# Two layers of a vision network on one core: attention sums two steps per instruction, normalized x kept in DRAM, weight loads regrouped over two queues

## The chip, the core and the metric

The kernel runs on one core of a Trainium2 chip. A core has five engines that run their own instruction streams: TensorE (PE in the profile; PEld is its weight load), VectorE (DVE), ScalarE (ACT), GpSimd (POOL) and SyncE (SP). SyncE, and also ScalarE, start transfers on DMA queues. Each queue's issuing engine works in order: an issue that waits for a semaphore holds back what stands behind it on that engine. SBUF is the on-chip memory, PSUM is where TensorE writes. The metric is the device time of one execution in microseconds; lower is better.

## The reference, cut to what matters

The input x is 2 images of 96 channels and 96 x 96 pixels, float32. Layer 0 is a selective scan (a state-space block) and a small feed-forward net, layer 1 is an attention and a feed-forward net. The change touches layer 0 only in how its weights are loaded. In layer 1 the attention counts:

```python
# layer 1, per image
xn = _ln_c(x)                       # normalized over the 96 channels
kv = einsum('oc,bchw->bohw', kv_w, xn)      # keys and values of all 9216 pixels
x_samp = mean of xn over 2 x 2 pixels       # 48 x 48 = 2304 cells
q_samp = einsum('oc,bchw->bohw', q_w, x_samp)
attn = softmax(k^T q * scale, over the 9216 pixels)   # 3 heads of 32
distribution = v attn                        # 96 x 48 x 48
lepe = depthwise 5 x 5 convolution of v + lepe_b
dmat = softmax(x_unfold . samp_unfold * dist_scale)   # each pixel, 3 x 3 cells
feature = dmat . unfold3(distribution)
x = x + proj_w (feature + lepe) + proj_b
x = x + ffn(layernorm(x))                    # quantized weights, relu
```

Of layer 0's weights, three matter here: dt_projs_bias (4 directions x 192 channels), A_logs (4 x 192 channels x 16 states) and dt_projs_weight.

## The kernel before, in words

**Order of work.** `_layer0` runs the whole first layer for both images and writes its result to the DRAM tile `x2d`. `_layer1` then takes one image after the other through three stages: `_l1_before` (norm, keys, queries, values), `_l1_attention` (which runs `_l1_packed`, or an arm that shifts the scores where a bound on them is large, which is not taken here), and `_l1_rows` (local 5 x 5 convolution, the 3 x 3 cells, projection, feed-forward net), eight times 12 rows. Pools are opened at the start of a stage and closed at its end; a pool that is opened later may lie on the memory of a closed one and then waits for its last readers.

**The planner.** Layer 0, the norm stage and the rows stage are written as operations with a cost, tiles read and written and a due time, and `_Plan` sorts them by list scheduling; `_in_order` then pins the issue order on every engine, SyncE included. DMA issues are operations of engine "sp" there. The attention is written out by hand, and only TensorE's order is pinned.

**The weights (`_l0_weights`).** SyncE issues every load in the order of the text: in_proj, off1, out_proj, norm weights, x_proj; then, for each of the four directions, two loads of dt_w (lines 323 and 324) and six of `dt_b`, 32 values each, straight into their interleaved places (lines 330 and 333); then 16 copies of A_logs into the DRAM tile `ad` (L381), one for each state, four reads of `ad` into `at0`, and Ds. VectorE reorders the reads of `ad` into `at` and TensorE transposes it (`pa`). VectorE also builds `selb`, `w_bc` and others from the identity and x_proj. Then `_layer0` opens its pools in the order front, hand, rep, back and the first load of x (`xt`, L464) is issued; the front's first matmul is `axc` (L475).

**The norm stage (`_l1_before`).** For each of 16 stripes of six rows SyncE loads x2d into `xt` (three buffers), TensorE, ScalarE and VectorE normalize it (`nxc`, `nva`, `rs`), and VectorE writes the result into its place in `xn`, an SBUF tile of the whole image (96 x 9216) that lives until the rows stage ends. Keys (`pk`), values (`pv`), queries (`pq`) and the 2 x 2 means (`xs`, GpSimd) are computed from it.

**Attention (`_l1_packed`).** The 48 x 48 cells go in five chunks: four of ten rows (480 cells), one of eight (384). The 72 blocks of 128 keys are spread over four strips of 32 partitions: strips 0 to 2 take the three heads' blocks 18 to 71 (54 steps), strip 3 takes the first 18 blocks of head 0, then of head 1, then of head 2 (18 steps each, index p). So a step has four score matmuls (L1382) into two PSUM tiles `sc`, two exponentials on ScalarE (L1386) into the SBUF tile `pr` of 4 x 480, four value matmuls (L1443) that add up in `av`, and on VectorE one addition of `pr` to `sums` (L1456). The order on TensorE is: scores of step j + 1, then values of step j. The first step of a chunk is a copy instead (L1451); the first step of p = 1 and p = 2 adds three strips and copies the fourth; the last step of each p adds strip 3's sums to those of head p. The closing of a chunk (`close`, a generator) is threaded into the next chunk's steps:

```python
            if rest and j in (2, 6):
                next(rest)
```

Ahead of step 0 ScalarE copies `av` to `avs`; at step 2 three matmuls with ones add the sums over the 128 partitions and VectorE takes the reciprocal; at step 6 five matmuls join strip 3's values to the heads and VectorE multiplies into `dist`.

**The rows stage (`_l1_rows`).** For 12 rows, `q` from 0 to 7: values again from `xn` (`pv2`, rows two above to two below), the score of each pixel with its cells (`st`, from `xs` and `xn`, L1574 to 1578), the exponentials multiplied by a mask on GpSimd, 20 taps of the 5 x 5 convolution on VectorE (`acc`, L1615) and five on TensorE, projection and feed-forward net, and on SyncE the loads of `xr` and the stores of `out`.

## Time and profile before

| What | us |
|---|---|
| three runs: median (lowest to highest) | 8884.31 (8876.86 to 8887.73) |
| the profiled execution | 8876.68 |
| its span, first to last instruction | 8874.9 |
| layer 0 with its weights | 0 to 6786 |
| image 0: norm stage, attention, rows stage | 6786 to 6862, to 7488, to 7830 |
| image 1: norm stage, attention, rows stage | 7830 to 7908, to 8535, to 8875 |
| busy over the span: TensorE, VectorE, ScalarE, GpSimd | 7426.3, 8093.4, 6381.7, 6189.7 |
| GpSimd and VectorE in layer 0, largest groups: h (L1050), h (L1045), bp (L1030) | 4120.9, 3998.7, 2173.8 |

The mean granted TensorE clock is 0.893 of full speed. The profile also gives: the span in 40 slices with the busy share of each engine, the chain of waits that ended last, groups of instructions by line (count, busy time, mean time of one, idle time ahead of them and who ended it), the same by stretch of time, and timelines. In a group "out<-in" are the program's tile names; "<-ACT pr L1386 3.3" says that 3.3 us of the idle time ahead of the group were ended by ScalarE's instruction on line 1386. In a table by stretch each engine has its busy time and its number of instructions.

### The profile page before, as it was taken

How to read it: one execution, taken by the hardware profiler on the slowest of the kernel's cores; microseconds unless marked ns; L12 is line 12 of the kernel's file. 1: busy time of each engine (PE TensorE's matmuls, PEld its weight loads, DVE VectorE, ACT ScalarE, POOL GpSimd, SP SyncE). 2: the span in 40 equal slices, each digit the busy share in tenths (PEclk: the TensorE clock that was granted, in tenths of full speed). 3: DMA queues.
4: the chain of work that ended last, by engine and by line, in shares of the span. 5: the costliest groups of instructions: out<-in, count | busy, mean ns of one | idle time of the engine just before them, and what ended most of it. 6: DMA issues, size and time to landing. Idle time of an engine off the chain costs nothing. (4 is left out here: it accounts for less than half of the span.)

```text
span 8874.9 us, 120352 instructions
## 1 busy us (share of the span) xinstructions
PE 7426.3 (84%) x43537; PEld 3500.8 (39%) x43537; DVE 8093.4 (91%) x5663; ACT 6381.7 (72%) x10720; POOL 6189.7 (70%) x3931
## 2 busy tenths in 40 slices
PE   6788888888788888888888888888856999989998
PEld 3333334444343344434444433443423333543345
DVE  2999999999999999999999999999996998969988
ACT  4677777777777777777777777777754876677766
POOL 3999999988999889899898889898974001310022
PEclk9899889999988888889898988888956999999999
DMA  2444444444444444444444444444441000010000
GB/s 77 140 143 145 148 142 143 145 142 140 144 142 141 147 142 144 142 146 143 143 142 144 144 139 143 144 140 144 144 131 55 2 2 5 24 28 3 2 10 24
DMA packets 335667, 969.48 MB, mean 109 GB/s; under 512 B 50424, under 2 KB 52144, under 8 KB 334768
## 3 DMA queue, kind: packets, MB, share of 16 engines
q1 hardware_dynamic: 335056, 961.64, 34.2%
q8 instruction: 346, 5.67, 0.3%
q14 instruction: 265, 2.17, 0.1%
HBM read 788.04 MB, written 132.17 MB: 104 GB/s over the span
## 5 line engine op out<-in xcount | busy, mean ns | idle before, releaser
L1050 POOL TENSOR_TENSOR h<-h,cre 128x864 f32<-128x864 f32 x2048 | 4120.9, 2021 | 684.6 <-DVE h L1045 488.5
L1045 DVE TENSOR_TENSOR_SCAN h<-dA,bp 128x864 f32<-128x864 f32 x2048 | 3998.7, 1953 | 83.5 <-PE y L1062 5.4
L1010 ACT ACTIVATE dA<-dlr,A 128x576 f32<-128x576 f32 x3072 | 2156.5, 765 | 1102.2 <-DVE h L1045 1015.6
L1030 DVE TENSOR_TENSOR bp<-dur,B 128x864 f32<-128x864 f32 x2048 | 2173.8, 1061 | 282.2 <-DMA dur<-du_d 42.3
L1062 PE MATMUL y<-h,fold 128*32 128x288 f32 (+2 forms) x18432 | 1870.3, 452 | 167.5 <-POOL h L1050 158.1
L1025 PE MATMUL B<-bt,selb 128*128 128x288 bf16 x2048 | 642.4, 315 | 957.6 <-DVE bp L1030 945.7
L536 PE MATMUL pc<-xin,off 96*96 96x288 f32 x4608 | 1331.0, 416 | 1.0 <-ACT xin L501 0.9
L1062 PEld LDWEIGHTS y<-h,fold 128*32 128x32 f32 x18432 | 762.2, 119 | 1140.4 <-issue 549.6
L1386 ACT ACTIVATE pr<-sc 128x960 f32<-128x960 f32 (+1 forms) x1080 | 955.1, 936 | 255.6 <-DVE sums L1456 144.5
L1456 DVE TENSOR_TENSOR sums<-sums,pr 128x1920 f32<-128x1920 f32 (+1 forms) x510 | 1059.2, 2077 | 58.2 <-ACT pr L1386 7.1
L1537 POOL MEMSET vch<- 96x32 f32 x16 | 2.0, 124 | 1313.8 <-DVE dist L1415 1265.8
L536 PEld LDWEIGHTS pc<-xin,off 96*96 96x96 f32 x4608 | 714.1, 166 | 506.3 <-issue 260.7
L1025 PEld LDWEIGHTS <-selb 128*128 128x128 bf16 x2048 | 200.6, 99 | 1312.3 <-DVE bp L1030 805.8
L1382 PE MATMUL sc<-qH,kH 32*128 32x480 f32 (+1 forms) x3240 | 708.3, 602 | 8.9 <-DMA q<-qH 8.9
L1382 PE MATMUL sc<-q,kH 32*128 32x480 f32 (+1 forms) x1080 | 564.5, 602 | 0.0
L1443 PE MATMUL av<-pr,vT 128*32 128x480 f32 (+1 forms) x4320 | 533.3, 564 | 3.8 <-ACT av L1460 3.5
L1615 DVE SCALAR_TENSOR_TENSOR acc<-vch,lepe_w,acc 96x1152 f32<-96x1152 f32 x304 | 485.7, 1598 | 7.6
L1382 PEld LDWEIGHTS sc<-qH,kH 32*128 32x128 f32 x3240 | 284.5, 184 | 437.5 <-issue 303.0
L709 PE MATMUL pt<-xd,w_dt 96*128 96x288 f32 x768 | 317.7, 507 | 22.9 <-ACT zs L519 10.6
L728 POOL TENSOR_TENSOR e<-e,du 128x576 f32<-128x576 f32 x192 | 271.1, 1412 | 26.6 <-ACT du L724 26.5
L1580 POOL TENSOR_TENSOR e<-e,mask 100x384 f32<-100x384 f32 x96 | 169.0, 1781 | 172.4 <-ACT e L1578 172.1
L730 POOL TENSOR_TENSOR dl<-dl,r 128x576 f32<-128x576 f32 x192 | 270.6, 1410 | 6.2
(260 smaller groups left out, 10113.7 us busy)
## 6 DMA issues: line engine op xcount, KB each, us to landing
cre<-c_d SPq DMA_DIRECT2D x1024, 288.0 KB
dur<-du_d SPq DMA_DIRECT2D x256, 864.0 KB
dlr<-dl_d SPq DMA_DIRECT2D x256, 864.0 KB
x<-xs SPq DMA_DIRECT2D x512, 72.0 KB
du_d<-du SPq DMA_DIRECT2D x128, 288.0 KB
dl_d<-dl SPq DMA_DIRECT2D x128, 288.0 KB
du_d<-du SPq DMA_DIRECT2D x128, 144.0 KB
dl_d<-dl SPq DMA_DIRECT2D x128, 144.0 KB
```

What stands on the lines that cost most here:

```text
L536: pe(H2, lambda: nc.tensor.matmul(pc.ap[:C, :H2], k.w_c1[:, ih, tap, oh * C : (oh + 1) * C], xin.ap[:, ih, 3 * c + dy : 3 * c + dy + 3, dx ...
L1010: nc.scalar.activation(dA.ap[:, :, blk, :], dlr.ap[:, blk, :].rearrange("p (c n) -> p c n", c=2), AF.Exp, scale=k.A[:, i, kg, h, blk : blk ...
L1025: nc.tensor.matmul(pB.ap[:, :H2], k.selb[:, kk, i, :], f.bc[o].ap[:, toks], start=True, stop=True)
L1030: nc.vector.tensor_tensor(bp.ap[:, : NBL * H2].rearrange("p (b n) -> p b n", b=NBL), dur.ap[:, :, toks], pB.ap[:, :H2].unsqueeze(1).to_bro ...
L1045: nc.vector.tensor_tensor_scan(hv, dv, bv, 0.0, ALU.mult, ALU.add)
L1050: nc.gpsimd.tensor_tensor(ht.ap, ht.ap, cre.ap[:, toks].unsqueeze(1).to_broadcast([128, NBL, H2]), ALU.mult)
L1062: nc.tensor.matmul(dst, k.fold, v, start=False, stop=stop)
L1382: nc.tensor.matmul(two[s // 2][:, s % 2, :n], kH[rows, k0 : k0 + 128], q, start=True, stop=True)
L1386: nc.scalar.activation(pr[:, 2 * i : 2 * i + 2, :n], two[i][:, :, :n], AF.Exp, scale=HD**-0.5)
L1443: nc.tensor.matmul((main if s < HEADS else other)[s * HD : (s + 1) * HD, :n], vT[:, blk, hd, :], pr[:, s, :n], start=at == 0, stop=at == e ...
L1456: nc.vector.tensor_tensor(sums[:, :, :n], sums[:, :, :n], pr[:, :, :n], ALU.add)
L1615: S.op("dve", 1.6, lambda: nc.vector.scalar_tensor_tensor(acc.ap, src(), W.lw[:, t : t + 1], acc.ap, ALU.mult, ALU.add), (vch,), (acc,))
```

## The change

It has four parts, made together.

1. *Weights.* `dt_b` is loaded with one transfer as `b` (96 x 4 x 2) and brought to its interleaved places by four small matmuls with 0/1 matrices that are cut from the identity (`take`, `take2`), and two copies. A_logs goes into `ad` with eight transfers, not 16. These, dt_w, `at0` and Ds are issued by ScalarE, the other loads by SyncE as before. `_layer0` opens its pools in the order rep, hand, back, front.
2. *Normalized x.* `xn` is no longer a tile of the image: the norm stage has it in its own working pool, and stores each stripe to the DRAM tile `xd`. The first 14 rows are loaded back into the small tile `xn0`; each 12 rows of the rows stage (q from 1) load their 16 rows (fewer at the edge) into one of two buffers.
3. *Sums in pairs.* `pr` holds two steps, `sums` two halves of five strips, and VectorE adds two steps in one instruction of 2 x 4 x 480. Strip 3's sums have a place at either end of `sums` (0 or 4), so that the four strips of a step lie side by side for each p: for even p the order of strips is 1, 2, 3, 0 with strip 3 first in memory (`strips`, `place`). The sum of strip 3 is then added on VectorE for p = 0 alone; for p = 1 and 2 the matmuls with ones take it in.
4. *The closing.* The matmuls with ones are ten in four rounds (the two halves, and strip 3 for heads 1 and 2), the first two rounds at step 2, the other two with the reciprocal at step 4; the joins and `dist` come at step 8. `avs` and `av3` have one buffer instead of two.

```diff
@@ -320,20 +320,33 @@
         rows = slice(kk * 6, kk * 6 + 6)
-        nc.sync.dma_start(dt_w[rows, o, kk, :], a["dt_w"][kg, :, 0:128])
-        nc.sync.dma_start(dt_w[rows, o, 2, kk * 64 : kk * 64 + 64], a["dt_w"][kg, :, 128:])
-        b = a["dt_b"]
-        for blk in range(2 * NBL):
-            half, r = divmod(blk, NBL)
-            src = b[r * CB : r * CB + CB, kg, half : half + 1]
-            if blk < 4:
-                nc.sync.dma_start(k.dt_b[blk::4, o, kk : kk + 1], src)
-            else:
-                r0 = kk * 64 + blk - 4
-                nc.sync.dma_start(k.dt_b[r0 : kk * 64 + 64 : 2, o, 2:3], src)
+        nc.scalar.dma_start(dt_w[rows, o, kk, :], a["dt_w"][kg, :, 0:128])
+        nc.scalar.dma_start(dt_w[rows, o, 2, kk * 64 : kk * 64 + 64], a["dt_w"][kg, :, 128:])
         for j in range(4):
...
+    b = tmp.tile([C, KG, 2], F32, tag="b", name="b")
+    nc.scalar.dma_start(b, a["dt_b"])
+    take = tmp.tile([C, 2, 128], F32, tag="take", name="take")
+    take2 = tmp.tile([C, 64], F32, tag="take2", name="take2")
+    nc.vector.memset(take, 0.0)
+    for blk in range(2 * NBL):
+        half, r = divmod(blk, NBL)
+        cols = k.ident[:C, r * CB : r * CB + CB]
+        nc.vector.tensor_copy(take[:, half, blk::4] if blk < 4 else take2[:, blk - 4 :: 2], cols)
+    ps.tile([128, 3, 512], F32, tag="beside", name="beside")
+    pb = ps.tile([128, 2, KG], F32, tag="pb", name="pb")
+    for half in range(2):
+        nc.tensor.matmul(pb[:, 0], take[:, half], b[:, :, half], start=half == 0, stop=half == 1)
+    nc.vector.tensor_copy(
+        k.dt_b[:, :, 0:2].rearrange("p o k -> p k o"), pb[:, 0].rearrange("p (k o) -> p k o", o=2))
+    for kk in range(2):
+        rows = slice(kk * 64, kk * 64 + 64)
+        nc.tensor.matmul(pb[rows, 1, :2], take2, b[:, 2 * kk : 2 * kk + 2, 1], start=True, stop=True)
+    nc.vector.tensor_copy(k.dt_b[:, :, 2], pb[:, 1, :2])
@@ -377,14 +390,15 @@
     src = a["A_logs"].rearrange("(n d) (k g) -> n d k g", n=NS, g=NG)
-    for n in range(NS):
-        nc.sync.dma_start(ad[n].rearrange("k (d g) -> d k g", g=NG), src[n])
+    dst = ad.rearrange("n k (d g) -> n d k g", g=NG)
+    for d in range(8):
+        nc.scalar.dma_start(dst[:, d], src[:, d])
     na = KG * 2 * NBL
...
     for i in range(NQ):
-        nc.sync.dma_start(
+        nc.scalar.dma_start(
             at0[i * na : (i + 1) * na], rows[i]
@@ -397,7 +411,7 @@
     ds4 = tmp.tile([C, KG, 2], F32, tag="ds4", name="ds4")
-    nc.sync.dma_start(ds4, a["Ds"])
+    nc.scalar.dma_start(ds4, a["Ds"])
     k.Dsum = cp.tile([C, 2], F32, tag="Dsum", name="Dsum")
@@ -1090,7 +1104,7 @@
             ffn = _ffn_weights(k, cp, tmp, "f0", a["W1_0"], a["b1_0"], a["W2_0"], a["b2_0"])
-        P.front, P.hand, P.rep, P.back = (pool(n, 1) for n in ("front", "hand", "rep", "back"))
+        P.rep, P.hand, P.back, P.front = (pool(n, 1) for n in ("rep", "hand", "back", "front"))
         P.ps = pool("ps0", 1, space=PSUM)
@@ -1131,7 +1145,8 @@
     held = lambda name: S.held(getattr(M, name), name)
-    xn, xs, kH, qH, vT, mk, mq = map(held, ("xn", "xs", "kH", "qH", "vT", "mk", "mq"))
+    xs, kH, qH, vT, mk, mq = map(held, ("xs", "kH", "qH", "vT", "mk", "mq"))
+    xn = S.tile(P.wk, [C, NTOK], "xn", 1)
@@ -1160,6 +1175,8 @@
             norm(c)
+        S.op("sp", 1.0, lambda: nc.sync.dma_start(
+            M.xd[:, s * T : (s + 1) * T], xn.ap[:, s * T : (s + 1) * T]), ((xn, s),), ())
         for n, f in enumerate((ALU.max, ALU.min)):
@@ -1363,7 +1381,10 @@
     cells = lambda m: slice(chunks[m][0] * CELLS, (chunks[m][0] + chunks[m][1]) * CELLS)
-    q3 = {}
+    q3, pairs = {}, {}
+    strips = lambda p: (0, 1, 2, 3) if p % 2 else (1, 2, 3, 0)
+    place = lambda s, p: s if p % 2 else (s + 1) % 4
@@ -1373,16 +1394,18 @@
         n, (p, t) = chunks[m][1] * CELLS, divmod(j, SHARED)
-        pr = wk.tile([128, 4, 480], F32, tag="pr", name="pr", bufs=3)
+        if j % 2 == 0:
+            pairs[m, j] = wk.tile([128, 2, 4, 480], F32, tag="pr", name="pr", bufs=3)
+        pr = pairs[m, j - j % 2][:, j % 2]
         two = [ps.tile([128, 2, 512], F32, tag="s", name="sc", bufs=3) for _ in range(2)]
-        for s in range(4):
-            rows = slice(s * HD, (s + 1) * HD)
+        for s in strips(p):
+            rows, to = slice(s * HD, (s + 1) * HD), place(s, p)
             k0 = (SHARED + j) * 128 if s < HEADS else (p * SHARED + t) * 128
...
             nc.tensor.matmul(
-                two[s // 2][:, s % 2, :n], kH[rows, k0 : k0 + 128], q, start=True, stop=True
+                two[to // 2][:, to % 2, :n], kH[rows, k0 : k0 + 128], q, start=True, stop=True
             )
-        for i in range(2):
+        for i in (0, 1) if p % 2 else (1, 0):
             nc.scalar.activation(
@@ -1391,15 +1414,20 @@
         n = chunks[m][1] * CELLS
-        avs = wk.tile([128, 480], F32, tag="avs", name="avs", bufs=2)
+        avs = wk.tile([128, 480], F32, tag="avs", name="avs", bufs=1)
         rden = wk.tile([C, 480], F32, tag="rden", name="rden", bufs=1)
...
         yield
-        for hd in range(HEADS):
-            nc.tensor.matmul(
-                av[hd * HD : (hd + 1) * HD, :n], k.ones[:, :HD], sums[:, hd, :n],
-                start=True, stop=True,
-            )
+        for r in range(4):
+            for hd in range(HEADS):
+                parts = [sums[:, u, v, :n] for v in ((1,), (2, 4), (3, 0))[hd] for u in range(2)]
+                if r < len(parts):
+                    nc.tensor.matmul(
+                        av[hd * HD : (hd + 1) * HD, :n], k.ones[:, :HD], parts[r],
+                        start=r == 0, stop=r == len(parts) - 1,
+                    )
+            if r == 1:
+                yield
         nc.vector.reciprocal(rden[:, :n], av[:C, :n])
@@ -1426,8 +1454,8 @@
         n = chunks[m][1] * CELLS
-        sums = wk.tile([128, 4, 480], F32, tag="sums", name="sums", bufs=2)
-        av3 = wk.tile([128, 2, 480], F32, tag="av3", name="av3", bufs=2)
+        sums = wk.tile([128, 2, 5, 480], F32, tag="sums", name="sums", bufs=2)
+        av3 = wk.tile([128, 2, 480], F32, tag="av3", name="av3", bufs=1)
         for j in range(steps):
@@ -1436,32 +1464,40 @@
             main, other = banks[m % 2], banks[(m + p) % 2]
-            for s in range(4):
+            for s in strips(p):
                 blk, hd = (SHARED + j, s) if s < HEADS else (t, p)
...
                     vT[:, blk, hd, :],
-                    pr[:, s, :n],
+                    pr[:, place(s, p), :n],
                     start=at == 0,
...
                 )
-            if j == 0:
-                nc.vector.tensor_copy(sums[:, :, :n], pr[:, :, :n])
-            elif t == 0:
-                nc.vector.tensor_tensor(sums[:, :3, :n], sums[:, :3, :n], pr[:, :3, :n], ALU.add)
-                nc.vector.tensor_copy(sums[:, 3, :n], pr[:, 3, :n])
-            else:
-                nc.vector.tensor_tensor(sums[:, :, :n], sums[:, :, :n], pr[:, :, :n], ALU.add)
+            if t % 2:
+                pr = pairs.pop((m, j - 1))
+                at = p % 2
+                if j == 1:
+                    nc.vector.tensor_copy(sums[:, :, :4, :n], pr[:, :, :, :n])
+                elif t == 1:
+                    heads = sums[:, :, 1 : 1 + HEADS, :n]
+                    nc.vector.tensor_tensor(heads, heads, pr[:, :, 1 - at : 4 - at, :n], ALU.add)
+                    nc.vector.tensor_copy(sums[:, :, 4 * at, :n], pr[:, :, 3 * at, :n])
+                else:
+                    both = sums[:, :, at : at + 4, :n]
+                    nc.vector.tensor_tensor(both, both, pr[:, :, :, :n], ALU.add)
             if t == SHARED - 1:
-                nc.vector.tensor_tensor(sums[:, p, :n], sums[:, p, :n], sums[:, 3, :n], ALU.add)
+                if p == 0:
+                    nc.vector.tensor_tensor(
+                        sums[:, :, 1, :n], sums[:, :, 1, :n], sums[:, :, 0, :n], ALU.add
+                    )
                 if p < 2:
...
                 load(m + (p + 2) // 3, (p + 2) % 3) if j > 1 or m else load(0, 2)
-            if rest and j in (2, 6):
+            if rest and j in (2, 4, 8):
                 next(rest)
@@ -1527,11 +1563,19 @@
     temp = lambda name: S.tile(P.wk, [C, T], name, 3)
-    xn, xs = S.held(M.xn, "xn"), S.held(M.xs, "xs")
+    xs = S.held(M.xs, "xs")
...
+    if q:
+        xn = S.tile(P.wk, [C, R + 4, HW], "xn", 2)
+        S.op("sp", 1.5, lambda: nc.sync.dma_start(
+            xn.ap[:, : min(R + 4, HW - y0)],
+            M.xd.rearrange("p (r w) -> p r w", w=HW)[:, y0 : min(y0 + R + 4, HW)]), (), (xn,))
+    else:
+        xn = S.held(M.xn0, "xn")
@@ -1548,7 +1592,7 @@
         op("pe", n, lambda: nc.tensor.matmul(
-            pv.ap[:C, :n], W.v, xn.ap[:, lo * HW : hi * HW], start=True, stop=True),
+            pv.ap[:C, :n], W.v, xn.ap[:, lo - y0 : hi - y0], start=True, stop=True),
             (xn,), (pv,), (vch,))
@@ -1564,7 +1608,7 @@
         j = 3 * q + i
-        toks = slice(j * 384, (j + 1) * 384)
+        toks = slice(4 * j - y0, 4 * j - y0 + 4)
         e = [S.tile(P.wk, [NEAR, 384], "e", 4) for _ in range(2)]
@@ -1737,7 +1781,7 @@
             nc.vector.tensor_tensor(W.pb, W.pb, pl[:C, 0:1], ALU.add)
-        img = pool("img", 1)
+        img, dram = pool("img", 1), pool("l1d", 1, space=DRAM)
@@ -1751,7 +1795,8 @@
             M = Ctx()
-            M.xn = img.tile([C, NTOK], F32, tag="xn", name="xn")
+            M.xd = dram.tile([C, NTOK], F32, tag="xd", name="xd")
+            M.xn0 = img.tile([C, 2 * WIN + 4, HW], F32, tag="xn0", name="xn0")
             M.xs = img.tile([C, CELLS + 2, CELLS + 2], F32, tag="xs", name="xs")
@@ -1764,6 +1809,9 @@
+                nc.sync.dma_start(
+                    M.xn0[:, 2:], M.xd[:, : (2 * WIN + 2) * HW].rearrange("p (r w) -> p r w", w=HW))
                 _l1_attention(k, tc, M)
```

## The prediction

> **What bounds the kernel now.** I read the page's 40 slices first: 31 are the first layer, and the built program's instruction order shows the first layer's steady work unchanged, engine by engine. So I read the three places that the diff touches: the weights ahead of the first layer, and, once per image, the stages of the second layer. First the busy time by stretch of image 0 (attention, the rows after it, the norm before it; engines PE, PEld, DVE, ACT, POOL, then granted clock):
>
> ```profile
> 6862.00:7488.00 626.00, 614.83 (x4400) 191.85 (x4400) 580.39 (x305) 485.00 (x555) 0.00 (x0) 0.98 0.01 3
> 7488.00:7830.00 342.00, 302.38 (x1145) 177.59 (x1145) 288.48 (x249) 219.12 (x470) 117.64 (x84) 0.93 0.07 21
> 6786.00:6862.00 76.00, 70.93 (x352) 50.30 (x352) 41.85 (x81) 59.59 (x155) 31.66 (x50) 0.95 0.19 51
> ```
>
> In attention VectorE is busy 580 of 626 us, at a clock of 0.98. The groups of that stretch by shape, then the timeline of VectorE:
>
> ```profile
> L1456 DVE TENSOR_TENSOR sums<-sums,pr 128x1920 f32<-128x1920 f32 x204 | 440.0, 2157 | 23.7 <-ACT pr L1386 3.3
> ...
> L1456 DVE TENSOR_TENSOR sums<-sums,pr 128x1536 f32<-128x1536 f32 x51 | 89.6, 1757 | 5.1
> ```
>
> ```profile
> 6875.44 36.10 DVE L1456 TENSOR_TENSOR sums<-sums,pr 128x1920 f32<-128x1920 f32 x16 [2.33 <-ACT pr L1386]
> ...
> 6994.64 1.15 DVE L1451 COPY sums<-pr 128x1920 f32<-128x1920 f32 x1
> ...
> 7120.53 1.15 DVE L1451 COPY sums<-pr 128x1920 f32<-128x1920 f32 x1
> ```
>
> Sixteen sums end 36.10 us after the first starts: (36.10 - 2.157) / 15 = 2.263 us apart, so 0.105 us lies between two. In the waits of ScalarE there, VectorE's sums are the largest item (19.0 us in 140). A chunk of ten rows (54 steps) takes 7120.53 - 6994.64 = 125.89 us. The two shapes give 400 ns for 384 elements, 1.042 ns each, and 157 ns whatever the size. What TensorE could do if VectorE did not hold it back shows after a chunk's end, where it catches up. The chain of waits there, in order of time:
>
> ```profile
> 6997.16 0.80 PE av L1399 x6
> 6997.96 1.02 PE sc L1382 x8
> 6998.98 0.94 PE av L1443 x8
> 6999.92 1.19 PE sc L1382 x8
> 7001.11 0.94 PE av L1443 x8
> ```
>
> and the same after the next-to-last chunk, where a chunk has 384 columns instead of 480:
>
> ```profile
> 7386.65 0.86 PE sc L1382 x8
> 7387.51 0.78 PE av L1443 x8
> 7388.29 1.03 PE sc L1382 x8
> ```
>
> Scores and values take 1.96 and 2.13 us in turn (1.02 or 1.19, and 0.94), so 2.045 us a step; at 384 columns 1.64 and 1.81. The second tile of scores waits for the exponentials of the step before, and that wait is not touched. So TensorE is only 10% behind VectorE: this decides the size of the gain.
>
> The start, from the timeline: VectorE's first scan (169.23 us) follows a serial front that begins when the image's first rows land:
>
> ```profile
> 27.28 10.90 SPq L381 DMA_DIRECT2D ad<-in_A_logs  x16
> ...
> 44.59 57.99 SPq L464 DMA_DIRECT2D xt<-in_x  x2
> ...
> 47.74 2.84 PE L475 MATMUL axc<-xt,less_mean 96*96 96x384 f32 x4 [5.22 <-DMA xt<-in_x]
> ```
>
> SyncE issues 53 small weight transfers between 4.75 and 40.4 us (the first line is 16 of them), and only then the load of x (44.59), so the front's first matmul starts at 47.74.
>
> **The change, part by part.**
>
> *Weights.* 24 loads of dt_b become one (plus four tiny matmuls, eight copies and a memset), 16 copies of A_logs become eight, and these with dt_w, Ds and at0 go to ScalarE's queue: 22 issues, at the rows' prices (10.90/16 = 0.68 for A_logs, 0.3 to 0.5 for the others, 1.58 for at0) 11 us. ScalarE's in-order queue stops once, at the eighth dt_w load: the built program gives the transfers of both queues eight semaphores in turn, and that one belongs to off1, which landed at 9.4 us (SyncE waited 4.3 us for it there). From 9.4: two dt_w, six A_logs, Ds are 5.3 us, the table load and bn_s 1.6, at0 1.6 and its landing 1.4: 19.3. Queued behind the dt_w loads on VectorE is now everything that needs ident: from 12.2 us about 11 us of small copies (selb 24 x 0.174, w_bc 1.6, others) lie ahead of the copy `at`: 23.2, then the transpose `pa`, which TensorE runs ahead of the front, 23.6. On SyncE, out_proj, bnv and f0w2 wait for ScalarE's transfers; x is issued behind Ds at about 17.5 and lands 3.1 us later (44.59 to 47.7): 20.6, hidden behind `pa`. The front starts at about 24 instead of 47.7: **-24 us**. Bounds: -18 if each shared-semaphore wait costs another landing, -30 if only ScalarE's chain binds. The new pool order lets the front's buffers not wait for the weights' memory; that is in the same 24.
>
> *Sums in pairs.* A sum of 3,840 elements: 157 + 4,000 = 4.157, and 0.105 after it, 4.262 against 2 x 2.262 = 4.524. A chunk on VectorE afterwards: 24 x 4.262 = 102.3; the first copy 2.26 (0.526 ns an element by the two copy rows); twice a sum of 2,880 (3.08) and a copy of 960 (0.70); one add of 960, 1.26; reciprocal and division 3.64. Sum 117.0. The same sum for before gives 126.6, 0.7 more than measured. TensorE's chunk: 54 x 2.045 = 110.4; ten matmuls with ones instead of three, four rounds instead of one (0.80, then 0.92 each as the joins there take) 3.6; five joins 4.5: 118.5, above VectorE. Following both through the closing (ones at steps 2 and 4, joins at 8), VectorE idles 0.5 us for the pair at step 4 and 2.1 us for the pair at step 10, and TensorE regains 0.17 us a pair to the end: 119.6, **6.3 us saved a chunk**. The first chunk saves 6.0 (the first pair waits for two steps). The last, of 384 columns: TensorE catches up there in steps of 1.64 and 1.81; 50 x 1.725, ones 3.5, joins 4.5, last exponentials and a last sum twice as long 5.4: 99.7 against 104.4, and 2.4 us more of ones exposed at the end: 2.3. An image saves 6.0 + 18.9 + 2.3 = 27.2, both **-54 us**. Bounds: VectorE alone (4 x 8.9 + 8.6 = 44 an image) -88; with a whole pair (4.1 us) lost at each closing on top of TensorE's 118.5, 14 an image, -28. I take the value between since both engines stand within 1.5 us of each other. The strips' new order keeps shapes, counts and waits: nothing. One buffer of avs and av3 instead of two adds waits on joins that ended 40 steps and 9 steps before: nothing.
>
> The Trainium skill, "VectorE: DVE Perf Modes", section "The TRN2 errata", has a rule that speaks against this part: the fixed cost, about 150 cycles, is paid once per instruction and is spread thin above 512 elements. The row's 157 ns agrees with the cost, but the 105 ns between two sums are no part of it: by the rule a pair would save 156 ns, an estimate from the page, VectorE's chunk would be 119.7, and the gain nearer 44 us than 54.
>
> *Normalized x in DRAM.* Per image 16 stores of 216 KB, one load for the first rows before attention, and seven of 576 KB in the rows stage. In the norm stage TensorE is busy 71 of 76 us and DMA share is 0.19, so bytes are covered. But each store stands on SyncE until VectorE's norm is done, with the next load of x queued behind; loads run up to three stripes ahead. I take +3 an image, **+6**; bounds 0 and +20 (ten us an image, a load's 2.71 us exposed four times). The first loads of x2d move behind the weights of layer 1 (issue 6784.2, landing 2.7, against a matmul at 6786.59): 0.3, inside that. xn0 is loaded in the middle of the stage, behind the third store's landing: hidden, and if it slipped to the end it would add its own 3 us ahead of the q3 loads. In the rows stage a load is issued once the rows two before are read, some 342/8 = 43 us ahead; it takes between 2.71 (a 216 KB load's row) and 7.2 us (scaled by size). Hidden; without that lead it would stand in full ahead of the scores of the next rows. The 24 new issues cost SyncE 0.3 us each, as its stores of out do (0.32), and SyncE is no bound. The order of the other work shifts: **+2**, bounds -10 and +16.
>
> Sum: -24 - 54 + 6 + 2 = -70 against the profiled execution's 8876.68 us (span 8874.9): 8806.7. That execution is 7.6 us below the median of 8884.31, at the lowest of the three runs; I give half of that back: **8810 us**.
>
> **The rivals.**
> *VectorE stays the bound.* For it: it is the releaser of ScalarE in every chunk now. Against: steps of 2.045. It gives -24 - 88 + 8 = -104: 8776.
> *The start's gain is lost* because the first scan waits for something else than the front. Against: no wait of the first 160 us but the front's own work follows 47.74. It gives -46: 8834.
> *Slower: the rows' loads come late.* One mechanism: SyncE runs in order, and a load of x for the next rows stands behind an output store that waits for POOL. For it: POOL's adds are the stores' releasers. Against: 43 us of lead. 14 loads at 5.1 us exposed eat the other 72 us; at 10 us (7.2 and a landing of 2.7) the kernel takes 8876.7 - 72 + 140 + 3.8 = 8949.
> *No difference*: the 32 stores hold back the norm's loads by 2.2 us each, 70 us: 8880.
>
> **How the numbers follow.** Chances: forecast 0.69, VectorE bound 0.16, start lost 0.05, late loads 0.07, no difference 0.03. Faster by over 0.2% (17.8 us, about what a measurement can tell from none) are the first three, 0.90; same 0.03; slower 0.07. The bounds of the parts together give 8752 (-30 - 88 + 0 - 10) to 8870 (-18 - 28 + 20 + 16); eight times in ten I expect 8770 to 8856, which leaves out late loads and the worst corner.
>
> **What would show it.** The front's first matmul at 21 to 27 us; chunk copies 118 to 121 us apart; the pair's sum at 4.16 us; idle time of the sums put down to ScalarE or TensorE some 2 to 3 us a chunk; the norm stage at 76 to 86 us, the rows at 335 to 355 with no wait of TensorE for xn. The prediction falls if chunks stay above 122 us, or if the rows stage shows waits for xn.

## The result, and the profile after

The changed kernel takes 8803.49 us (median of 4 runs, 8800.41 to 8804.93) against 8884.93 (4 runs, 8876.86 to 8887.73): 81.4 us less, a ratio of 0.9909 with a 95% interval of 0.9892 to 0.9927. The forecast was 8810. The profiled execution of the changed kernel took 8803.46 us, its span is 8801.6, so the two profiles differ by 73.3 us: the profiled execution of before was one of its quickest.

The spans cut at the same landmarks, in us (landmarks: VectorE's first `bp`, GpSimd's last `h`, the first `nxc` and the first `sc` of each image, the start of the last `dist` of each image):

| Stretch | before | after | difference | forecast |
|---|---|---|---|---|
| start to VectorE's first scan step | 169.2 | 144.4 | -24.8 | -24 |
| from there to GpSimd's last h | 6572.1 | 6576.5 | +4.4 | 0 |
| to the first `nxc` of the norm stage | 45.3 | 44.7 | -0.6 | 0 |
| both norm stages, up to the first scores | 156.3 | 158.3 | +2.0 | +6 |
| both attentions, up to the last `dist` | 1246.4 | 1188.8 | -57.6 | -54 |
| both rows stages (with the step to the next stage) | 685.7 | 689.0 | +3.3 | +2 |
| sum | 8874.9 | 8801.6 | -73.3 | -70 |

The start first. The timeline of ScalarE's and SyncE's queues and of TensorE in the changed kernel (start, duration, engine, line, what, what it had waited for):

```profile
9.35 0.27 ACTq L324 DMA_DIRECT2D dt_w<-in_dt_w  x1
10.36 3.81 ACTq L395 DMA_DIRECT2D ad<-in_A_logs  x6
```

```profile
9.78 0.31 SPq L272 DMA_DIRECT2D out_proj<-in_out_proj  x1
...
16.82 0.31 SPq L478 DMA_DIRECT2D xt<-in_x  x1
```

```profile
22.24 0.39 PE L406 MATMUL pa<-ident,at 96*128 96x96 f32 x1 [7.59 <-DVE Dsum L417]
23.02 2.85 PE L489 MATMUL axc<-xt,less_mean 96*96 96x384 f32 x4 [0.39 <-ACT A L409]
```

ScalarE's queue stops until 9.35 us at its ninth issue, the sixth dt_w load (the forecast said the eighth); x is issued at 16.82, the transpose `pa` runs at 22.24 and the front's first matmul at 23.02 instead of 47.74. `pa` and not the load of x is what the front now stands behind: the gap ahead of `axc` is 0.39 us.

Then attention. The groups of VectorE in image 0 by shape (count, busy, mean ns of one, idle ahead and who ended it):

```profile
L1489 DVE TENSOR_TENSOR sums<-sums,pr 128x3840 f32<-128x3840 f32 x96 | 399.0, 4156 | 23.0 <-ACT pr L1409 13.3 <-DVE sums L1486 0.5 <-DVE sums L1489 0.5
L1489 DVE TENSOR_TENSOR sums<-sums,pr 128x3072 f32<-128x3072 f32 x24 | 80.5, 3356 | 6.1 <-ACT pr L1409 4.0
...
L1482 DVE COPY sums<-pr 128x3840 f32<-128x3840 f32 x4 | 8.6, 2154 | 11.0 <-ACT pr L1409 11.0
```

A sum of two steps takes 4.156 us where two sums took 2 x 2.157. VectorE's timeline at the closing of the first chunk, and two later chunk copies:

```profile
6969.47 2.15 DVE L1482 COPY sums<-pr 128x3840 f32<-128x3840 f32 x1
6971.72 4.16 DVE L1489 TENSOR_TENSOR sums<-sums,pr 128x3840 f32<-128x3840 f32 x1
6976.29 4.16 DVE L1489 TENSOR_TENSOR sums<-sums,pr 128x3840 f32<-128x3840 f32 x1 [0.41 <-ACT pr L1409]
6980.37 3.15 DVE L1431 RECIPROCAL rden<-av 96x480 f32<-96x480 f32 x1
6983.43 8.35 DVE L1489 TENSOR_TENSOR sums<-sums,pr 128x3840 f32<-128x3840 f32 x2
6991.71 0.65 DVE L1443 TENSOR_TENSOR dist<-av,rden 96x480 f32<-96x480 f32 x1
6994.65 16.95 DVE L1489 TENSOR_TENSOR sums<-sums,pr 128x3840 f32<-128x3840 f32 x4 [2.30 <-ACT pr L1409]
...
7088.59 2.15 DVE L1482 COPY sums<-pr 128x3840 f32<-128x3840 f32 x1
...
7208.05 2.15 DVE L1482 COPY sums<-pr 128x3840 f32<-128x3840 f32 x1
```

Four sums that start at 6994.65 end 16.95 later: (16.95 - 4.156) / 3 = 4.26 us apart. VectorE idles 0.41 us ahead of the pair at step 4 and 2.30 ahead of the one at step 10, both times for ScalarE's exponentials. From copy to copy a chunk takes 119.12 (6969.47 to 7088.59), then 119.46; before it was 125.89. The waits of ScalarE over a chunk and a bit (6990 to 7130 us; us in total, times, longest) have changed hands. Before, most of its waiting was for VectorE's sums; in the changed kernel it is for TensorE's scores:

```profile
ACT pr L1386 <- DVE sums L1456: 19.0, 39, 2.8
ACT pr L1386 <- PE sc L1382: 6.4, 9, 2.1
```

```profile
ACT pr L1409 <- PE sc L1405: 22.9, 42, 4.8
```

### The profile page after: what moved, and what is told of

Its sections match the earlier page's. It is cut to its first block, busy times and chain, and to the rows that moved or that the text cites. A ratio compares the mean times of both kernels' runs of the same rounds, so it can differ in the third digit from the quotient of the medians.

```text
span 8801.6 us, 119886 instructions
## 1 busy us (share of the span) xinstructions
PE 7370.6 (84%) x43685; PEld 3443.1 (39%) x43685; DVE 8030.7 (91%) x5382; ACT 6380.5 (72%) x10720; POOL 6185.3 (70%) x3931
## 5 line engine op out<-in xcount | busy, mean ns | idle before, releaser
L1489 DVE TENSOR_TENSOR sums<-sums,pr 128x3840 f32<-128x3840 f32 (+1 forms) x240 | 959.1, 3996 | 57.9 <-ACT pr L1409 34.7
L1405 PE MATMUL sc<-qH,kH 32*128 32x480 f32 (+1 forms) x3240 | 627.6, 602 | 10.4 <-DMA q<-qH 10.4
L1405 PEld LDWEIGHTS sc<-qH,kH 32*128 32x128 f32 x3240 | 219.2, 184 | 420.7 <-issue 222.2
L841 ACT CAST fh<-fph 128x288 f16<-128x288 f32 x384 | 141.4, 391 | 186.3 <-PE fph L838 185.6
```

Source lines behind the costliest of these rows:

```text
L1405: nc.tensor.matmul(two[to // 2][:, to % 2, :n], kH[rows, k0 : k0 + 128], q, start=True, stop=True)
L1489: nc.vector.tensor_tensor(both, both, pr[:, :, :, :n], ALU.add)
```

## The experiments

**The start: which of its parts does it.** Three kernels have only the weights changed. `start_alone` is part 1 of the change on the kernel before. `one_queue` is the same with every `nc.scalar.dma_start` of the weights turned into `nc.sync.dma_start`. `old_pools` is part 1 without this line:

```diff
-        P.front, P.hand, P.rep, P.back = (pool(n, 1) for n in ("front", "hand", "rep", "back"))
+        P.rep, P.hand, P.back, P.front = (pool(n, 1) for n in ("rep", "hand", "back", "front"))
```

> Only the weights of layer 0 and the order of its pools are changed; attention and xn stay as before. Theory: this part is worth what the front gains. The front's first matmul is at 23.0 us as in the kernel after (47.74 before), VectorE's first scan at 144.4 (169.23 before), so 25 us by then; the time falls by 20 to 25 us, to 8860 to 8865. Rival A: the first layer takes back a part: between the first scan and GpSimd's last h the kernel after took 6576.5 us and the kernel before 6572.1, 4.4 us more; if the change does that, the same 4.4 us show here, and if it is scatter from execution to execution they need not. Rival B: the start was not the limit and nothing is gained: 8885.

> As the start alone, but every transfer is issued by SyncE: fewer transfers, no second queue. Theory: both halves count. Before, 53 small issues lie between 4.75 and 40.4 us; 23 of dt_b at 0.6 us with gaps (2.40 for 4, 1.24 for 2: 14 us) and 8 of A_logs at 0.68 (5.4 us) go, 19 us, so x is issued at about 25 to 26 instead of 44.6 and the front's first matmul is at 28 to 30 (first scan 149 to 152). Rival A: fewer transfers do all of it: the front at 23, first scan 144.4. Rival B: the second queue does it all: the front at 45 or later.

> The start alone, with layer 0's pools opened in the old order (front, hand, rep, back), so that the front's first tiles lie where the weights' temporary tiles lay. Theory: the load of x then waits for the weights' last readers there; in the kernel before, x was issued 1.9 us after the queue was free (42.65 to 44.59), 2.4 us behind the transpose pa. With pa at 22.1 as in the start alone, x is issued at 24 to 25 and lands 3.1 us later: the front's first matmul at 27 to 28.5 instead of 22.9, the first scan about 5 us later. Rival: the pools' order has no effect on the start: 22.9, first scan 142.4 to 144.4.

`start_alone`: 8856.17 us (8 runs) against 8881.51 (17 runs, 8869.11 to 8889.23), 25.3 us less, ratio 0.9975 (0.9964 to 0.9985); first matmul of the front 22.90, first scan 142.4. Of `one_queue` and `old_pools` there is one execution each, so they are read by their timelines. TensorE's start in `one_queue`, and in `old_pools`:

```profile
22.61 0.39 PE L406 MATMUL pa<-ident,at 96*128 96x96 f32 x1 [3.31 <-DVE at L404]
25.20 2.85 PE L489 MATMUL axc<-xt,less_mean 96*96 96x384 f32 x4 [2.20 <-DMA xt<-in_x]
```

```profile
22.39 0.39 PE L406 MATMUL pa<-ident,at 96*128 96x96 f32 x1 [7.58 <-DVE Dsum L417]
26.57 2.85 PE L489 MATMUL axc<-xt,less_mean 96*96 96x384 f32 x4 [3.79 <-DMA xt<-in_x]
```

With one queue the front starts at 25.20, 2.3 us later than with two: x is issued at 21.86 and TensorE waits 2.20 us for it. With the old order of pools x is issued at 23.30, after `pa`, and the front starts at 26.57, 3.7 us later. So fewer transfers with the new order of pools bring 22.5 of the front's 24.8 us (47.74 to 25.20), and the second queue 2.3; with both queues, the old order of pools takes 3.7 back. How the 22.5 split between fewer transfers and the pools' order no run shows: there is none with one queue and the old order. The expectation for one queue, 28 to 30, was too late: it counted 19 us of issues that go; in the timeline of before the four groups of dt_b issues take 14.9 us and A_logs 5.7 more than here, 20.6, and the wait of 1.9 us for the weights' memory goes as well.

**The 4.4 us of the first layer.** The stretch from first scan to last h has the same code in all kernels. It took 6572.1 us before and 6576.5 after. With the old start it took 6569.9 in `xn_alone` and 6579.7 in `xn_and_pairs` (both below), with the new start alone 6573.2 in `start_alone`, 6568.3 in `one_queue` and 6576.2 in `old_pools`: nothing here speaks for a cost of the new start. In the other kernels told of below, which all sum in pairs, it takes 6575.9 to 6581.1. That could look like a cost of the pairs, since all nine kernels with pairs lie at 6575.9 or more and four of the five without lie below. But each figure is one execution, and these executions lie differently in their kernels' scatter: those of before, `start_alone` and `xn_alone` took 8.2, 4.9 and 3.2 us less than their kernels' medians, that of `xn_and_pairs` 3.5 more. An estimate that puts these distances into this stretch gives 6580, 6578, 6573 and 6576 us, against 6576.5 after: then nothing is left of the 4.4 us. That the distances arise in this stretch no run shows, so the cause stays open.

**x in DRAM.** `xn_alone` is part 2 alone on the kernel before; `one_xn` is the whole change with one buffer for the loads of the rows stage:

```diff
-        xn = S.tile(P.wk, [C, R + 4, HW], "xn", 2)
+        xn = S.tile(P.wk, [C, R + 4, HW], "xn", 1)
```

> Only the normalized x goes to DRAM; weights and attention as before. Theory: the stores and loads are hidden: norm stage and rows stage cost 2 to 8 us in all over both images (the kernel after showed 0.6 and 1.4 in the norm stages, 1.0 and 2.3 in the rows stages), so 8886 to 8893. Rival: the loads of xn are late in the rows stage, 5 us or more for each of 14: 8955 or more, with TensorE waiting for xn. Attention unchanged: chunk copies 125.9 us apart.

> The kernel after with one buffer for xn in the rows stage instead of two: the load for the next 12 rows can start only when the last read of these is done, instead of some 43 us ahead of its use. Theory (the lead of two buffers hides the loads): now each of 14 loads shows with 1 to 7 us, the planner hiding a part behind other work: the rows stages 10 to 90 us longer together, with TensorE waiting for xn, 8815 to 8890. Rival (the loads are hidden anyhow, the lead is not what matters): the rows stages within 5 us, 8800 to 8808.

`xn_alone`: 8881.15 us (10 runs) against 8881.51, ratio 1.0 (0.999 to 1.0009), that is 9 us less to 8 us more: the 32 stores and 16 loads cost nothing that can be measured. `one_xn`: 8803.80 us (4 runs, 8800.92 to 8807.26), the same as with two buffers, so the theory that the lead of 43 us is what hides the loads falls. SyncE's queue and TensorE around one of its loads:

```profile
7529.65 0.30 SPq L1574 DMA_DIRECT2D xn<-xd  x1
```

```profile
7528.81 0.81 PE L1618 MATMUL st<-xn,xs 96*100 96x384 f32 x2
7538.42 2.14 PE L1594 MATMUL pv<-xn,v_w 96*96 96x384 f32 x6
```

The load is issued at 7529.65, right after the last scores that read the buffer (7528.81), and the next rows' values start at 7538.42 with no wait named: the planner puts other work between. 8.8 us are enough for the 576 KB.

**Do the parts add up.** `xn_and_pairs` is the change without part 1.

> Normalized x in DRAM and sums in pairs, with the weights loaded as before. Theory: the parts add up. Attention saves 28 and 30 us as in the kernel after (chunk copies 119.1 us apart), the norm and rows stages cost 5: 8884.9 - 53 = 8832, and this with the start alone (-21 to -25) gives the whole change (-81 by medians, -73 by the two profiles). Rival: the parts lean on each other (the new start moves the first layer and with it the stages after it): the two do not add up to the whole within 10 us.

8823.18 us (4 runs) against 8881.51: -58.3, ratio 0.9933 (0.9917 to 0.995). With the start's -25.3 that is -83.6 against -81.4 for the whole: the parts add up, closer than these measurements can tell (the intervals allow 13 to 32 us for the start and 44 to 74 for the rest). Parts 3 and 4 of the change were not run apart from each other.

**Who sets the pace in attention.** Two kernels take work from one engine each, on the changed kernel; a third undoes the turned strips.

`three_ones`, in `close`:

```diff
                 parts = [sums[:, u, v, :n] for v in ((1,), (2, 4), (3, 0))[hd] for u in range(2)]
+                parts = parts[:1]
                 if r < len(parts):
```

> The kernel after, with only the first three of the ten matmuls with ones (the sums of the second half and of strip 3 for heads 1 and 2 are left out of the denominators). It takes TensorE's work away and leaves VectorE's. In the kernel after the two groups of ones take 1.81 and 1.60 us of a chunk in the chain of waits; 0.8 stays, so 2.6 us go from TensorE. Theory (TensorE sets the pace, VectorE close behind: its own work sums to 116.4 us a chunk of 119.1, idle 0.4 and 2.3 at the closing): chunk copies 116.5 to 117.2 us apart. Rival (VectorE still sets the pace): they stay 119.1 apart.

`fewer_sums`, in the chunk loop:

```diff
-                else:
+                elif t != 9:
                     both = sums[:, :, at : at + 4, :n]
```

> The kernel after, with three of a chunk's 24 full sums in pairs left out (the tenth pair of steps of each p does not count in the denominators). It takes 3 x 4.26 = 12.8 us of a chunk from VectorE and nothing from TensorE. Theory (TensorE sets the pace, and waits 1.4 us a chunk for VectorE, at the ones and at the copy of av): chunk copies 117.7 to 119.1 us apart. Rival (VectorE sets the pace): the chunk falls with VectorE's work, to between 106 and 110.

VectorE's copies at the start of the third and fourth chunk, in `three_ones` and then in `fewer_sums`:

```profile
7094.52 2.15 DVE L1483 COPY sums<-pr 128x3840 f32<-128x3840 f32 x1
...
7211.62 2.15 DVE L1483 COPY sums<-pr 128x3840 f32<-128x3840 f32 x1
```

```profile
7091.06 2.15 DVE L1482 COPY sums<-pr 128x3840 f32<-128x3840 f32 x1
...
7210.41 2.15 DVE L1482 COPY sums<-pr 128x3840 f32<-128x3840 f32 x1
```

With 2.6 us taken from TensorE the chunk falls from 119.1 to 116.7 and 117.1 (the last is 7094.52 to 7211.62); with 12.8 us taken from VectorE it does not fall: 119.3 to 119.6 in image 0. TensorE sets the pace of every chunk with a closing in it. VectorE's own 116.4 us (119.1 less the two idle times of 0.41 and 2.30) stand just beneath. The first chunk of an image has no closing of a chunk before it, and there VectorE counts: first copy to second takes 118.7 us after, 114.0 in `fewer_sums`, 4.7 of the 12.8 us less.

`plain_strips` has four places in `sums` instead of five:

```diff
-    strips = lambda p: (0, 1, 2, 3) if p % 2 else (1, 2, 3, 0)
-    place = lambda s, p: s if p % 2 else (s + 1) % 4
+    strips = lambda p: (0, 1, 2, 3)
+    place = lambda s, p: s
...
-        sums = wk.tile([128, 2, 5, 480], F32, tag="sums", name="sums", bufs=2)
+        sums = wk.tile([128, 2, 4, 480], F32, tag="sums", name="sums", bufs=2)
...
-                if p == 0:
-                    nc.vector.tensor_tensor(
-                        sums[:, :, 1, :n], sums[:, :, 1, :n], sums[:, :, 0, :n], ALU.add
-                    )
+                nc.vector.tensor_tensor(
+                    sums[:, :, p, :n], sums[:, :, p, :n], sums[:, :, 3, :n], ALU.add
+                )
```

> Sums in pairs without the turned strips: strip 3 always lies last, sums has four places, its sum is added to the head's after each p, and six matmuls with ones stand in two rounds. VectorE gets two adds of 960 more (1.16 + 0.1 each, 2.5 us a chunk: 118.9), TensorE loses two rounds of ones (about 1.6 us: 117.5). Theory (both engines within a few us of each other, so the greater counts): VectorE becomes the bound, with idle time at the closing on top: chunk copies 119.5 to 121.5 us apart, 0 to 20 us slower in all than the kernel after (8803 to 8823). Rival (TensorE alone sets the pace): 117.5 apart, 13 us faster than the kernel after.

8815.47 us (4 runs, 8808.57 to 8819.49), ratio 0.9919 (0.9902 to 0.9935). The chunk copies are 119.86 us apart (7099.58 to 7219.44):

```profile
7099.58 2.15 DVE L1480 COPY sums<-pr 128x3840 f32<-128x3840 f32 x1
...
7219.44 2.15 DVE L1480 COPY sums<-pr 128x3840 f32<-128x3840 f32 x1
```

2.5 us more for VectorE and 1.6 less for TensorE make the chunk 0.4 to 0.7 us longer. By the sums (118.9 against 117.5) VectorE is the bound here. The expected range of the chunk held; in the times the intervals of the two kernels overlap, so what the turned strips are worth in all is not measured.

**A faster version, two failures first.** If TensorE sets the pace at the closing, its ones and joins are the place. GpSimd does nothing in attention, so `pool_merge` has it add up the halves and strip 3's sums. The ones then come at step 12 and the joins at step 14:

```diff
+            add = lambda a, b: nc.gpsimd.tensor_tensor(a, a, b, ALU.add)
+            add(sums[:, 0, :, :n], sums[:, 1, :, :n])
+            add(sums[:, 0, 2, :n], sums[:, 0, 4, :n])
+            add(sums[:, 0, 3, :n], sums[:, 0, 0, :n])
+            add(sums[:, 0, 1, :n], first[:, :n])
...
-        for r in range(4):
+        for r in range(4 if end else 1):
...
-            if rest and j in (2, 4, 8):
+            if rest and j in (2, 12, 14):
```

> The kernel after, with GpSimd, idle in attention, adding up the halves and strip 3's sums at the end of chunks 1 to 4, so that three matmuls with ones in one round are enough there and VectorE's add after p = 0 goes; in the last chunk the joins go into the free bank ahead of the ones. TensorE 119.3 - 2.6 = 116.7 a chunk, VectorE 116.4 - 1.3 = 115.1. Theory (TensorE sets the pace): chunk copies 116.4 to 117.2 us apart, the tail after the last sum 3 to 5 us shorter, 25 to 32 us less in all: 8772 to 8779. Rival (GpSimd's additions slow VectorE's sums beside them, or the ones wait for GpSimd): sums of more than 4.2 us there, chunks at 118 or more, 8790 or more.

`no_joins` also takes the five joins from TensorE, with three small transfers and an add on GpSimd:

```diff
                     nc.scalar.copy(av3[last, p, :n], other[last, :n])
+                    nc.sync.dma_start(moved[p * HD : (p + 1) * HD, :n], av3[last, p, :n])
...
+        nc.sync.dma_start(moved[2 * HD : C, :n], avs[last, :n])
+        add(moved[:, :n], avs[:C, :n])
...
-            av[:C, :n].rearrange("p (r w) -> p r w", w=CELLS),
+            moved[:, :n].rearrange("p (r w) -> p r w", w=CELLS),
```

> As the former, and the join of strip 3's values to the heads leaves TensorE too: three small transfers a chunk move them to the heads' partitions, GpSimd adds them to the copy of av, VectorE multiplies from SBUF. TensorE 116.7 - 4.5 = 112.2 a chunk, VectorE 115.1 as before. Theory: the bound goes over to VectorE: chunk copies 115.1 to 116.2 us apart, the tail after the last sum 6 to 7 us shorter than in the kernel after (no joins between reciprocal and dist): about 40 us less than the kernel after, 8758 to 8770. Rival (TensorE's steps set the pace whatever is taken from the closing, through the exponentials): chunks stay at 116.5 or more, 8770 to 8780.

Both lost. `pool_merge`: 8904.36 us (10 runs), ratio 1.0024 (1.0014 to 1.0034), slower than before the change. `no_joins`: 8818.51 (4 runs), 0.9926 (0.9909 to 0.9942); its interval overlaps the changed kernel's, but its chunks are longer, 124.8 us against 119.1. VectorE's timeline in `pool_merge` at two closings (6967 and 7104) and in between, then GpSimd's:

```profile
6967.58 2.15 DVE L1497 COPY sums<-pr 128x3840 f32<-128x3840 f32 x1
6969.84 14.14 DVE L1504 TENSOR_TENSOR sums<-sums,pr 128x3840 f32<-128x3840 f32 x2
...
7025.37 4.11 DVE L1500 TENSOR_TENSOR sums<-sums,pr 128x2880 f32<-128x2880 f32 x1 [0.26 <-ACT pr L1409]
7104.26 9.08 DVE L1504 TENSOR_TENSOR sums<-sums,pr 128x3840 f32<-128x3840 f32 x1
```

```profile
6967.81 17.22 POOL L1438 TENSOR_TENSOR sums<-sums 128x2400 f32<-128x2400 f32 x3 [72.70 <-DVE sums L1504]
6984.99 5.11 POOL L1438 TENSOR_TENSOR sums<-sums,first 128x480 f32<-128x480 f32 x1
7025.26 1.21 POOL L1507 TENSOR_TENSOR first<-sums 128x480 f32<-128x480 f32 x1 [35.15 <-DVE sums L1504]
```

One sum in pairs takes 9.08 us beside GpSimd's additions (7104.26) where it takes 4.16 alone, and two take 14.14. GpSimd is slowed as well: an add of 480 takes 5.11 us among sums (6984.99). Where such an add starts first, at 7025.26, it takes 1.21, and VectorE's sum of 2,880, which starts 0.11 us later (7025.37), takes 4.11 instead of 3.16. The chunks with a closing are 133 to 135 us long in both images.

Longer instructions of VectorE are about half of what these chunks have over 119.1. `no_joins` gives GpSimd the same additions and one more, and its chunk is 124.8: VectorE is busy for 122.1 us of it, in `pool_merge` for 121.2 of 134.4, in the changed kernel for 114.0 of 119.1. What `pool_merge` has on top is a wait of TensorE. Its joins write the tile that the reciprocal reads, and the reciprocal stands behind the late sums:

```profile
7005.77 1.80 PE L1426 MATMUL av<-avs,join 128*32 128x480 f32 x2 [7.59 <-DVE rden L1452]
```

Around this wait TensorE is slow as well: its granted clock is 0.61 from 7002 to 7022 us and 1.00 from 7040 to 7100; `no_joins`, which has no joins on TensorE, has 0.91 from 7002 to 7022. VectorE then idles 4.83 us for the joins and 5.74 for the exponentials. At the next two closings of this image the clock is 0.63 and 0.66. So the rival with contention was right. Two things were the mistake: to count an idle engine's time as free, and to let TensorE wait for the reciprocal at step 14.

`two_joins` keeps GpSimd out. The three transfers stay; in chunks 1 to 4 two matmuls of 96 rows replace the five joins, in the last chunk VectorE adds:

```diff
+        if end:
+            whole = moved
+            nc.vector.tensor_tensor(moved[:, :n], moved[:, :n], avs[:C, :n], ALU.add)
...
+        if not end:
+            for i, part in enumerate((avs, moved)):
+                nc.tensor.matmul(
+                    av[:C, :n], k.ident[:C, :C], part[:C, :n], start=i == 0, stop=i == 1)
```

> The kernel after, without GpSimd's help. Three small transfers a chunk bring strip 3's values to the heads' partitions; in chunks 1 to 4 two matmuls of 96 rows with the identity (0.9 us each, as the joins) then stand in place of the five joins, in the last chunk VectorE adds (0.6 us) behind its last sum, while TensorE does the ones. TensorE 119.3 - 2.7 = 116.6 a chunk, VectorE 116.4 as in the kernel after. Theory (TensorE sets the pace, and beside GpSimd's adds VectorE was only held up by them): chunk copies 116.6 to 117.6 us apart, from the last sum's end to dist 5 to 7 us less than in the kernel after, sums of 4.16 throughout; 20 to 32 us less than the kernel after in all: 8771 to 8784. Rival (the three transfers or VectorE's own closing take the gain back): chunks at 118.5 or more, 8790 or more.

8769.14 us (4 runs, 8756.70 to 8772.86) against 8882.22 (7 runs), ratio 0.9868 (0.9852 to 0.9885): faster than both kernels, and 34 us below the changed one (20 to 32 were expected). VectorE's timeline, two chunk copies and the tail of image 0 after the last sum:

```profile
7097.44 2.15 DVE L1483 COPY sums<-pr 128x3840 f32<-128x3840 f32 x1
...
7214.53 2.15 DVE L1483 COPY sums<-pr 128x3840 f32<-128x3840 f32 x1
...
7400.19 27.61 DVE L1490 TENSOR_TENSOR sums<-sums,pr 128x3072 f32<-128x3072 f32 x8 [0.42 <-ACT pr L1409]
7427.78 0.55 DVE L1425 TENSOR_TENSOR moved<-moved,avs 96x384 f32<-96x384 f32 x1
7432.19 2.55 DVE L1436 RECIPROCAL rden<-av 96x384 f32<-96x384 f32 x1 [3.86 <-PE av L1430]
7434.78 0.56 DVE L1443 TENSOR_TENSOR dist<-moved,rden 96x384 f32<-96x384 f32 x1
```

117.1 us a chunk (7097.44 to 7214.53; the two beside it 116.7), and 7.0 us from the end of the last sum (7427.80) to `dist`. In the changed kernel that tail is 12.8 us (7426.40 to 7439.24), 7.25 of which is `dist` waiting for the joins (the same view):

```profile
7398.80 27.60 DVE L1489 TENSOR_TENSOR sums<-sums,pr 128x3072 f32<-128x3072 f32 x8 [0.42 <-ACT pr L1409]
7429.44 2.55 DVE L1431 RECIPROCAL rden<-av 96x384 f32<-96x384 f32 x1 [3.04 <-PE av L1425]
7439.24 0.56 DVE L1443 TENSOR_TENSOR dist<-av,rden 96x384 f32<-96x384 f32 x1 [7.25 <-PE av L1435]
```

The sums take 4.16 us again. This confirms from the other side that TensorE's closing is what the changed kernel's attention waits for.

## Why the prediction was right, point by point

- *The start, -24*: step for step nearly as written: the stop at 9.35 us, x issued at 16.8 (17.5 forecast), `pa` 22.2 (23.6), the front 23.0 (24). That the first scan then came 24.8 us earlier is in part luck: in the nine kernels with this start the front begins at 22.9 to 23.1 us, but the first scan anywhere from 140.6 to 150.2. What the forecast left unsplit, the runs split: fewer transfers and the pools carry it, the second queue is worth 2.3 us.
- *A sum in pairs 4.157 us, 4.262 to the next*: 4.156 and 4.26. The rows had the price in them. The Trainium skill, "VectorE: DVE Perf Modes", section "The TRN2 errata", has a fixed cost of about 150 cycles for each instruction and no figure for the gap between two. An estimate that saves this cost alone gives 4.37 from one sum to the next; the measured 4.26 shows that the gap is saved too.
- *A chunk of 119.6, TensorE above VectorE*: 119.1 to 119.5. TensorE's 118.5 is 119.4 where VectorE is relieved, VectorE's 117.0 is 116.4, and the idle times of 0.5 and 2.1 at the closing are 0.41 and 2.30. The rival "VectorE stays the bound" falls by `fewer_sums`. Here the mechanism was right and not only the number.
- *First and last chunk*: both terms were off, in opposite directions. From the first score to the second copy 4.8 and 5.6 us were saved in the two images (6.0 forecast), in the last chunk with its tail 3.2 and 4.1 (2.3). The middle chunks saved 20.0 an image (18.9).
- *Normalized x, +6 and +2*: +2.0 and +3.3 by the two profiles; the runs of `xn_alone` show nothing, though their interval reaches to 8 us. The +3 an image for stores that stand on SyncE ahead of loads was the mis-sized term: the norm stages grew by 0.6 and 1.4 us. The rival "late loads" needed 5.1 us at each of 14 loads; there is no wait for xn, not even with one buffer.
- *From the profile to the median*: the sum was made against an execution 7.6 us below the median, and half of that was given back. The changed kernel's profile lies at its median (8803.46 and 8803.49), so the whole difference should have been given back to the gain: -81.4 by medians, -73.3 by profiles.
- *The sum, -70*: that it lies 3.3 us from the -73.3 is helped by luck. The first layer's +4.4, which nobody forecast, stands against 3.6 us more gained in attention and 2.7 less lost in the norm and rows stages.

## What to carry to other kernels

Two shapes of one instruction gave its fixed cost and its cost per element here, and a timeline gave the gap between two; from these the price of the merged instruction came out to a few ns. Before an engine is relieved, work out how far the next one stands behind it: here merging took 9.5 us of a chunk's 125.9 from VectorE, TensorE let 6.4 to 6.8 of it through, and the next gain lay in TensorE's closing. An idle engine is not free room: before work is moved to it, measure how long its instructions and its neighbour's take when they run side by side.

## What the runs showed of the hardware that was not expected

GpSimd and VectorE hold each other up when both add tensors in SBUF: 9.08 instead of 4.16 us for a sum of 3,840 elements, 5.11 instead of 1.21 for GpSimd's add of 480. The pair at 7025 shows the order: the add that starts first keeps its 1.21 us, and the sum that starts 0.11 us later takes 0.95 us more than alone, about the 1.10 us that are left of the add. The Trainium skill, "SBUF — State Buffer", section "Who interferes with whom", says this for a VectorE instruction with two SBUF inputs beside a GpSimd instruction that reads SBUF: the later one blocks until the first is done. The rows of `pool_merge` agree with it, and it speaks against `pool_merge` from the start.

TensorE ran slower around its long waits. In `pool_merge` its granted clock was 0.61, 0.63 and 0.66 in the 20 us around the wait for the reciprocal at three closings of image 0, and 1.00 in stretches of 60 to 74 us between them. Two matmuls of the joins take 1.80 us there (7005.77); in the changed kernel, at a clock of 1.00, they take 0.97 (6985.13). That the wait brings the clock down was not tested by itself.

Of the start: most of the gain does not need a second queue. 31 transfers fewer on one queue, with the new order of pools, bring 22.5 of the front's 24.8 us, and splitting the rest over two queues 2.3.
